# A state space block on Trainium2: the causal convolution as four shifted projections

## The chip, the core and the metric

The kernel runs on one core of one Trainium2 chip. The metric is the device time of one execution in microseconds (us); smaller is better. A core has a matrix engine (TensorE, "PE" in the profile, with "PEld" for its loading of weights), a vector engine (VectorE, "DVE"), a scalar engine (ScalarE, "ACT"), GpSimd ("POOL") and SyncE ("SP", which here issues most of the DMA transfers). Each engine works through its own queue of instructions in order; semaphores tie the queues together.

## The reference

The program is a network of four blocks on an activation `x` of shape (4, 1024, 128) in f32: four batches of 1024 tokens with 128 features. Each block is an attention-like part and a feed-forward part, each followed by `x = layernorm(x + f(x))`: block 0 is a minimal GRU with a slot feed-forward, block 1 a sparse attention with a routed feed-forward, block 2 a linear attention with a mixture of 8 experts (two per token), and block 3 a state space block with a feed-forward of 8 dense experts of hidden width 512. The change lies in block 3:

```python
def _L3_attn_ref(resid, norm_w, skip_w, in_w, conv_w, conv_b, wd1, wd2, wd2_b, wb, wc, A_log, W_D, out_w):
    ...
    x = resid * lax.rsqrt(jnp.mean(resid * resid, -1, keepdims=True) + EPS) * norm_w
    skip = x @ skip_w.T
    xe = x @ in_w.T                       # 128 features -> E = 256 channels
    xt = xe.transpose(0, 2, 1)
    xc = lax.conv_general_dilated(xt, conv_w, window_strides=(1,), padding=[(D_CONV - 1, 0)],
                                  feature_group_count=conv_w.shape[0])
    xc = xc + conv_b[None, :, None]
    xs = jax.nn.silu(xc.transpose(0, 2, 1))
    delta = jax.nn.softplus(xs @ wd1.T @ wd2.T + wd2_b)
    A = -jnp.exp(A_log)
    Bm = xs @ wb.T
    Cm = xs @ wc.T
    ...
    # for each of N = 16 states: h = exp(delta*A)*h + delta*xs*B, y = sum of h*C   (a scan over time)
    y = ys.transpose(1, 0, 2)
    y = y + xs * W_D
    y = y * jax.nn.silu(skip)
    y = y @ out_w.T
    return resid + y
```

The convolution has width 4, is causal (each output takes the token itself and the three before it, zeros ahead of the first) and depthwise: each of the 256 channels has its own four weights.

## The kernel before

**Order.** The kernel is written in the Tile framework. The Python text emits instructions in program order, interleaving several generators; a scheduler (`schedule_with_timeline_sim=True`, L2133) then fixes each engine's in-order queue from a simulated timeline. So the place of an instruction in its queue follows from what it depends on and from the durations that the scheduler assumes, not from the text alone. Only the PE order within `l2_attn` is written by hand (L962). Buffers come from pools: a tile name with `bufs=n` has n buffers used in turn, and a new tile waits until the last reader of the buffer it takes is done.

**Stages.** `Net.__init__` (L63 to L85) loads constants; the front (blocks 0 and 1, with the GRU first, its gates on ACT, its scans on DVE) takes roughly the first 620 us. `l2_attn` (L919) does the linear attention in quarters of 256 tokens with eight pairs of heads each. Its values are made in `l2_values` (L1014): for each of two 128-token chunks a tile `cv1` ("cv" in the profile) from a pool with two buffers gets a column of ones by POOL (L1019), its sums with the bias by DVE (L1029), and is then scaled by ACT (L1036) into its final form. `l2_ffn` (L1377) and `l2_combine` (L1494) are the mixture of experts of block 2, per batch: a dispatch with rows scattered into DRAM by POOL's indirect DMAs (`xrows`, L1359), tiles of tokens with their expert weights `wx` loaded by SP (L1433), and gathers of the results (`yrows` to `yg`, L1504) by POOL. They are drawn as a generator `moe` and run on into the last stage.

**The last stage, `l3` (L1549).** It works in eight halves: four batches times two halves of 512 tokens. Channels lie on partitions, in two blocks of 128 (`ec`), time lies along the free axis. A half has these steps:

- `l3_prepare` (L1652): the RMS norm of four 128x128 tiles, four transposes, an eviction by ACT with the norm's weight into `xnT` (128 features x 512 tokens, L1676). For each block one f32 matmul makes `pxe` (128 x 512 in PSUM, L1687); the helper `mm` (L127) issues every matmul, which is why so many groups carry that line. The convolution then reads `pxe`: DVE writes weight 3 times `pxe` plus the bias to `xc` (L1693) and adds the other three taps, each a `scalar_tensor_tensor` on columns shifted by 1, 2 and 3 (L1699). The three columns that the second half of a batch needs from the first are kept, already weighted, in a tile `tail` (L1697 and L1703 to L1710). All weights are halved in advance (`cw`), so that ACT's tanh (L1713, back into the PSUM bank) and one DVE operation (L1714) give the SiLU, `xs`. Two matmuls make `pdb` (64 delta features, B and C rows), which ACT evicts to `db1` (L1722) and SP writes to DRAM as `rows`; two more make `pd`, from which Exp, Ln and six-odd DVE operations make the softplus, with `ud` (delta times xs, L1748, DVE) and `dl` (delta, L1749, ACT) as results.
- `l3_scan` (L1752), for each of 16 states: SP broadcasts one row of B and one of C over 128 partitions (`bn`, `cn`, L1777); POOL multiplies `db = ud*bn` (L1782); ACT makes the decay `da` (L1786) and DVE scans `db` in place (L1787); in the first half of a batch ACT keeps the last column in `carry` (L1796); POOL multiplies `hc = db*cn` (L1798). Every second `hc` of batches 1 to 3 is added to its neighbour by an accumulating DMA that POOL issues (L1802); the rest is summed by identity matmuls into `pys`.
- `l3_sum` (L1811) and `l3_finish` (L1823): `xs` becomes `pys` plus xs times W_D (L1819), `psk` is the skip projection of the same `xnT`, `po` the output projection, then layer norm and router.
- `l3_experts` and `l3_ffn` (L1604, L1892): for each half, 8 experts of four 512-column matmuls `ph`, a ReLU `hh` on ACT (L1910), sixteen 128-column matmuls `py`, and DVE's gated sum `h_acc` (L1926). Their weights `wh` come by SP (L1639), three buffers.

`l3` weaves these: with each of the 16 scan steps of a half goes one step of the previous half's end, one step of the next half's preparation, one step of `moe`, and three or four steps of the experts. What is left of the experts runs at the very end on PE, which then has all eight PSUM banks. Before that, PSUM has one bank for each of two `pys`, two for `da`, and four under the name "ff" for everything else, `pxe`, `pdb`, `pd`, `ph` and `py` alike (L1641).

Of the kernel before, what the change touches and what calls it, by code (L numbers as in the profile page):

```python
# [18 lines left out]
P = 128  # L19
# [13 lines left out]
NH2, HD2 = 16, 64  # L33
VW = HD2 + 1
# [6 lines left out]
E3, NST, DDELTA, KCONV = 256, 16, 64, 4  # L41
# [17 lines left out]
class Net:  # L59
# [954 lines left out]
    def l2_values(self, Q):  # L1014
        nc, c2 = self.nc, self.c2
        wp = c2["wp"]
        for c in range(2):
            v1 = wp.tile([P, NH2, VW], F32, name="cv1")
            nc.gpsimd.memset(v1[:, :, HD2 : HD2 + 1], 1.0)  # L1019
            for g in range(2):  # L1020
                pv = self.psb("pj", [P, 8, HD2], "pv")
                gs = slice(g * 512, g * 512 + 512)
                self.mm(
                    pv.rearrange("p h d -> p (h d)"),
                    Q["x"][:, c * P : (c + 1) * P],
                    c2["wv"][:, gs],
                )
                hs = slice(8 * g, 8 * g + 8)
                nc.vector.tensor_add(  # L1029
                    v1[:, hs, 0:HD2],  # L1030
                    pv,
                    c2["bv"][:, gs].rearrange("p (h d) -> p h d", d=HD2),
                )
                k = Q["c0"] + c
                for i in range(2):
                    nc.scalar.activation(  # L1036
                        Q["v"][c][:, hs, i, :],
                        v1[:, hs, :],
                        AF.Copy,
                        scale=c2["trig"][:, k, i : i + 1],  # L1040
                    )
                yield
# [489 lines left out]


    def l3_load(self):
        return dict(
            wskip=self.load("s_in", [P, 2, E3]),
            we=self.load("s_e", [P, 2, ND + D]),
            wd2=self.load("s_d2", [DDELTA + 1, E3]),
            br=self.load_row("h_br", NE),
            wr=self.load("h_router", [P, NE]),  # L1540
            b2=self.load("h_b2", [NE, D]),
        )
# [6 lines left out]
    def l3(self, w3, moe, fp):  # L1549

        nc, tc, c = self.nc, self.tc, self.const
        aneg = c.tile([P, 2 * NST], F32, name="aneg")
        o = COLS["A_log"][0]
        nc.scalar.activation(aneg, self.cols[:, o : o + 2 * NST], AF.Exp)
        nc.vector.tensor_scalar_mul(aneg, aneg, -1.0)

        o, n = COLS["conv_w"][0], 2 * KCONV + 2  # L1560
        cw = c.tile([P, n], F32, name="cw")
        nc.vector.tensor_scalar_mul(cw, self.cols[:, o : o + n], 0.5)
        c3 = self.c3
        neg1 = c.tile([P, 1], F32, name="neg1")
        nc.vector.memset(neg1, -1.0)
        c3.update(w3, aneg=aneg, cw=cw, neg1=neg1)
        halves = [dict(b=b, h=h) for b in range(B) for h in range(2)]
        for i, u in enumerate(halves):
            u["prev"] = halves[i - 1] if u["h"] else None
        while "done" not in self.m2["st"][0]:  # L1570
            next(moe)
        for f in self.l3_prepare(halves[0]):
            next(moe)
        work = self.l3_experts(fp)
        c3["todo"] = []
# [24 lines left out]
        c3["all"] = True  # L1600
        for f in work:
            pass
# [49 lines left out]
    def l3_prepare(self, u):  # L1652

        nc, c3, b, h = self.nc, self.c3, u["b"], u["h"]
        sp, wp, dp = c3["sp"], c3["wp"], c3["dp"]
# [16 lines left out]
        pt = self.psb("ff", [P, 4, P], "pt")  # L1672
        for k in range(4):
            self.tr(pt[:, k, :], sq[:, k, :])
        xnT = wp.tile([P, 512], F32, name="xnT")
        nc.scalar.activation(  # L1676
            xnT, pt.rearrange("p a b -> p (a b)"), AF.Copy, scale=self.col("norm_w")
        )
        yield

        K1 = KCONV - 1
        tail = wp.tile([P, 2, K1], F32, name="tail") if h == 0 else u["prev"]["tail"]
        u["tail"] = tail
        xs = wp.tile([P, 2, 512], F32, name="xs3")
        for ec in range(2):
            p = self.psb("ff", [P, 512], "pxe")
            self.mm(p, c3["wskip"][:, 1, ec * P : (ec + 1) * P], xnT)  # L1687
            xc = sp.tile([P, 512], F32, name="xc", tag="s1")
            i = 2 * KCONV + ec
            w = [c3["cw"][:, j : j + 1] for j in range(ec * KCONV, (ec + 1) * KCONV)]  # L1690
            bias = c3["cw"][:, i : i + 1]
            o = K1 if h else 0
            nc.vector.tensor_scalar(xc[:, o:], p[:, o:], w[K1], bias, ALU.mult, ALU.add)  # L1693
            if h:
                nc.vector.scalar_tensor_tensor(
                    xc[:, 0:K1], p[:, 0:K1], w[K1], tail[:, ec, :], ALU.mult, ALU.add
                )  # L1697
            for d in range(1, KCONV):
                nc.vector.scalar_tensor_tensor(  # L1699
                    xc[:, d:], p[:, 0 : 512 - d], w[K1 - d], xc[:, d:], ALU.mult, ALU.add  # L1700
                )
            if h == 0:
                nc.vector.tensor_scalar(  # L1703
                    tail[:, ec, :], p[:, 512 - K1 :], w[0], bias, ALU.mult, ALU.add
                )
                for d in range(K1 - 1, 0, -1):
                    nc.vector.scalar_tensor_tensor(
                        tail[:, ec, 0:d], p[:, 512 - d :], w[K1 - d], tail[:, ec, 0:d],
                        ALU.mult, ALU.add,
                    )  # L1710
            yield

            nc.scalar.activation(p, xc, AF.Tanh)  # L1713
            nc.vector.scalar_tensor_tensor(xs[:, ec, :], p, 1.0, xc, ALU.add, ALU.mult)  # L1714
            yield

# [2 lines left out]
        p = self.psb("ff", [ND, 512], "pdb")  # L1719
# [23 lines left out]
        for ec in range(2):  # L1743
            p = p2[ec]
# [78 lines left out]
    def l3_finish(self, u):  # L1823


        nc, c3, b, h = self.nc, self.c3, u["b"], u["h"]
        sp, wp = c3["sp"], c3["wp"]
# [2 lines left out]
        yt = u["xs"]  # L1830
        for ec in range(2):
            p = ff([P, 512], "psk")
            self.mm(p, c3["wskip"][:, 0, ec * P : (ec + 1) * P], u["xnT"])

            t = sp.tile([P, 512], F32, name="th")
            nc.scalar.activation(t, p, AF.Tanh, scale=0.5)
            nc.vector.scalar_tensor_tensor(p, t, 1.0, p, ALU.add, ALU.mult)
            nc.vector.scalar_tensor_tensor(
                yt[:, ec, :], yt[:, ec, :], 0.5, p, ALU.mult, ALU.mult
            )  # L1840
            yield
# [18 lines left out]
        n = NC // 2  # L1860
# [89 lines left out]
    ("p_bq", 1), ("p_bk", 1), ("p_bv", 1), ("h16", 1),  # L1950
    ("f_b1", 12), ("f_b2", 2), ("f_sb2", 1),
    ("c_bq", NP2), ("c_bk", NP2),
    ("norm_w", 1), ("conv_w", 2 * KCONV), ("conv_b", 2), ("A_log", 2 * NST),
    ("one64", 1),
    ("W_D", 2),
    ("h_b1", 4 * NE),
# [1 line left out]
COLS, NCOLS = {}, 0  # L1958
# [25 lines left out]
def layout(i):  # L1984
# [5 lines left out]
    a = constants()  # L1990
    a["x"] = i["L0_attn_x"]

    cols = {}
# [7 lines left out]
    s = {k[len("L0_ffn_") :]: v for k, v in i.items() if k.startswith("L0_ffn_")}  # L2001
# [15 lines left out]
    s = {k[len("L1_attn_") :]: v for k, v in i.items() if k.startswith("L1_attn_")}  # L2017
# [6 lines left out]
    s = {k[len("L1_ffn_") :]: v for k, v in i.items() if k.startswith("L1_ffn_")}  # L2024
# [13 lines left out]
    s = {k[len("L2_attn_") :]: v for k, v in i.items() if k.startswith("L2_attn_")}  # L2038
# [23 lines left out]
    cols["one64"] = np.arange(P) == DDELTA  # L2062
    a["s_d2"] = np.concatenate([s["wd2"].T, s["wd2_b"][None, :]])
    cols["norm_w"], cols["conv_b"] = s["norm_w"], s["conv_b"]
    cols["conv_w"] = s["conv_w"].reshape(2, P, KCONV).transpose(0, 2, 1).reshape(-1)
    cols["A_log"] = s["A_log"].reshape(2, P, NST).transpose(0, 2, 1).reshape(-1)
    cols["W_D"] = s["W_D"]

# [68 lines left out]
```

## Time and profile before

Three runs took 2418.57, 2433.83 and 2437.38 us. The profiled execution is a further one.

| | |
|---|---|
| median of the three runs | 2433.83 us |
| the profiled execution's own time | 2426.07 us |
| its span in the profile | 2424.3 us, 35395 instructions |
| mean granted TensorE clock | 0.914 of full speed |
| PE busy | 2077.0 us (86%), 12170 instructions |
| PEld busy | 1456.7 us (60%) |
| DVE busy | 1439.7 us (59%), 4207 instructions |
| ACT busy | 1335.6 us (55%), 2934 instructions |
| POOL busy | 860.8 us (36%), 557 instructions |
| DMA | 209.87 MB, 75 GB/s to and from HBM over the span |

How to read what follows. The span is what the profiler's records cover; the execution's own time is 1.8 us longer. An f32 matmul leaves two matmul records and two weight loads, so counts (x) of PE are twice the matmuls in the text. Records of PE overlap their neighbours in the pipeline and their ends are modelled, so their durations add up to more than the time that PE takes for them. In the slices, the span is cut into 40 equal parts and each digit gives the busy share in tenths. A row for a window gives each engine's busy time and count, the granted clock of PE (1 is full speed), the mean busy share of the 16 DMA engines and the bytes they moved. A row of the chain of waits gives start, length, engine, what was made, the line, and a count: the chain is followed back from the last instruction to whatever released each step. A row for one instruction gives start and duration, and in brackets how long its engine stood idle before it and what ended that. A row of a tile's operations gives count, then least, median and greatest duration in ns, then the first and last start, then shapes.

### The profile page before, as it was taken

Reading aid. Unit: us, or ns where it says so; the run is one execution under the profiler, and the core shown is the slowest. Engines: PE = TensorE matmul, PEld = TensorE weight load, DVE = VectorE, ACT = ScalarE, POOL = GpSimd, SP = SyncE. Lnnn points to the kernel's source line nnn. Section 1 sums busy time; section 2 is a strip of 40 time slices with the busy share of each in tenths; the row PEclk is TensorE's granted clock in tenths of the full one; section 3 lists DMA queues with packets and bytes.
Section 4 is the critical chain, followed back from the end, with each engine's and each line's share of the span. In section 5 each row is a group of like instructions: output and inputs, shape, how many; then the busy total and the mean of one; then the engine's idle time right before and its main releaser. Section 6 shows DMA issues by size and latency. Waiting matters only on the chain. (4 is left out here: it accounts for less than half of the span.)

```text
span 2424.3 us, 35395 instructions
## 1 busy us (share of the span) xinstructions
PE 2077.0 (86%) x12170; PEld 1456.7 (60%) x12170; DVE 1439.7 (59%) x4207; ACT 1335.6 (55%) x2934; POOL 860.8 (36%) x557
## 2 busy tenths in 40 slices
PE   6767979979899999999989865776788989798988
PEld 3455655544577777787768754553455656465666
DVE  6457733433466666755656556676778777676431
ACT  6543433332456565656655555657677776666443
POOL 5001220000000011001021137868899979688500
PEclk9657969989999999999989988997999989898999
DMA  3000110013000010021222156663577766575421
GB/s 101 0 18 21 29 33 7 12 64 92 1 1 1 1 33 22 16 76 41 62 74 82 42 158 190 210 181 91 147 187 185 201 165 184 149 205 151 113 66 48
DMA packets 138517, 209.87 MB, mean 87 GB/s; under 512 B 18598, under 2 KB 75937, under 8 KB 138081
## 3 DMA queue, kind: packets, MB, share of 16 engines
q1 hardware_dynamic: 126048, 172.82, 24.0%
q0 software_dynamic: 12288, 34.79, 6.8%
q8 instruction: 96, 1.57, 0.3%
q14 instruction: 85, 0.69, 0.1%
HBM read 159.24 MB, written 23.16 MB: 75 GB/s over the span
## 5 line engine op out<-in xcount | busy, mean ns | idle before, releaser
L1798 POOL TENSOR_TENSOR hc<-db,cn 128x1024 f32<-128x1024 f32 x128 | 317.2, 2501 | 81.1 <-PE pys L127 29.7
L1782 POOL TENSOR_TENSOR db<-ud,bn 128x1024 f32<-128x1024 f32 x128 | 326.0, 2574 | 44.1 <-ACT dl L1749 16.4
L127 PEld LDWEIGHTS py<-wh,hh 128*128 128x128 f32 x2048 | 249.5, 193 | 78.2 <-issue 43.7
L127 PE MATMUL ph<-xT,wh 128*128 128x512 f32 x512 | 262.7, 632 | 24.8 <-DVE h_acc L1926 7.5
L1145 DVE SCALAR_TENSOR_TENSOR num<-po,sb_c_trig,nsin 128x65 f32<-128x65 f32 x512 | 132.7, 279 | 232.1 <-ACT nsin L1142 218.3
L127 PE MATMUL py<-wh,hh 128*128 128x128 f32 x2048 | 255.9, 277 | 13.0 <-ACT hh L1910 12.7
L1910 ACT ACTIVATE hh<-ph,sb_cols 128x512 f32<-128x512 f32 x256 | 171.1, 681 | 137.7 <-PE ph L127 111.5
L1142 ACT ACTIVATE nsin<-po,sb_c_trig 128x65 f32<-128x65 f32 x512 | 148.3, 316 | 176.7 <-DVE num L1145 103.5
L1786 ACT ACTIVATE da<-dl,aneg 128x512 f32<-128x512 f32 x256 | 175.4, 689 | 74.6 <-DVE db L1787 72.8
L1019 POOL MEMSET cv<- 128x16 f32 x32 | 4.0, 127 | 497.7 <-ACT cv L1036 354.8
L127 PE MATMUL pys<-hc,sb_c_ident 128*128 128x512 f32 x320 | 164.3, 642 | 14.7 <-DMA hc<-hc 14.7
L127 PEld LDWEIGHTS ph<-xT,wh 128*128 128x128 f32 x512 | 92.6, 201 | 117.5 <-issue 63.9
L1926 DVE SCALAR_TENSOR_TENSOR h_acc<-py,gt,h_acc 128x128 f32<-128x128 f32 x256 | 71.9, 343 | 153.0 <-PE py L127 145.3
L1787 DVE TENSOR_TENSOR_SCAN db<-da,carry,db 128x512 f32<-128x512 f32 x128 | 156.8, 1266 | 5.9 <-ACT da L1786 4.3
L1787 DVE TENSOR_TENSOR_SCAN db<-da,db 128x512 f32<-128x512 f32 x128 | 149.8, 1206 | 11.3 <-ACT da L1786 10.1
L127 PE MATMUL pqk<-xT,wE 128*128 128x256 f32 x512 | 137.0, 391 | 7.4 <-DVE cv L1029 6.0
L1359 POOL DMA_INDIRECT xrows<-xN,di x64 | 61.9, 968 | 221.2 <-ACT kN L1063 216.4
L1109 PE MATMUL po<-cv,a 128*128 128x130 f32 x1024 | 136.9, 276 | 0.9 <-DVE num L1145 0.9
L1109 PEld LDWEIGHTS po<-cv,a 128*128 128x128 f32 x1024 | 125.5, 192 | 2.6 <-issue 1.0
L1036 ACT ACTIVATE cv<-cv,sb_c_trig 128x520 f32<-128x520 f32 x128 | 86.4, 724 | 51.4 <-DVE cv L1029 46.0
L127 PEld LDWEIGHTS pys<-hc,sb_c_ident 128*128 128x128 f32 x320 | 61.1, 203 | 80.4 <-issue 59.1
L127 PEld LDWEIGHTS pqk<-xT,wE 128*128 128x128 f32 x512 | 87.9, 191 | 25.3 <-DVE cv L1029 10.1
(430 smaller groups left out, 4440.4 us busy)
## 6 DMA issues: line engine op xcount, KB each, us to landing
wx<-in_wF SPq DMA_DIRECT2D x92, 384.0 KB
wh<-in_wH SPq DMA_DIRECT2D x64, 512.0 KB
bn<-rows SPq DMA_DIRECT2D x128, 256.0 KB
cn<-rows SPq DMA_DIRECT2D x128, 256.0 KB
hc<-hc POOLq DMA_DIRECT2D x48, 512.0 KB
xrows<-zero SPq DMA_DIRECT2D x4, 1472.0 KB
xg<-xrows SPq DMA_DIRECT2D x20, 256.0 KB
yrows<-ys SPq DMA_DIRECT2D x20, 256.0 KB
```

The lines of the kernel that those rows point to most:

```text
L127: return self.nc.tensor.matmul(out=out, lhsT=lhsT, rhs=rhs, start=start, stop=stop)
L1036: nc.scalar.activation(Q["v"][c][:, hs, i, :], v1[:, hs, :], AF.Copy, scale=c2["trig"][:, k, i : i + 1],)
L1109: self.nc.tensor.matmul(out=u["po"][i][:, c, :], lhsT=u["a"][:, i, c, :], rhs=Q["v"][c][:, 2 * hp + i, :, :].rearrange("p a d -> p (a d)") ...
L1142: nc.scalar.activation(t, po[i][:, c, VW : 2 * VW], AF.Copy, scale=trig[:, k, 1:2])
L1145: nc.vector.scalar_tensor_tensor(num[:, c, i, :], po[i][:, c, 0:VW], trig[:, k, 0:1], t, ALU.mult, ALU.add)
L1359: i = nc.gpsimd.indirect_dma_start(out=rows[:, :], out_offset=bass.IndirectOffsetOnAxis(ap=st["dest"][k][:, c : c + 1], axis=0), in_=self. ...
L1782: nc.gpsimd.tensor_mul(db, ud, bc[0])
L1786: nc.scalar.activation(da, dl[:, ec, :], AF.Exp, scale=aneg[:, j : j + 1])
L1787: nc.vector.tensor_tensor_scan(db[:, ec, :], da, db[:, ec, :], carry[:, ec, n : n + 1] if h else 0.0, ALU.mult, ALU.add,)
L1798: nc.gpsimd.tensor_mul(hc, db, bc[1])
L1910: nc.scalar.activation(ht, ph, AF.Relu, bias=self.col("h_b1", i=e * NK + k))
L1926: nc.vector.scalar_tensor_tensor(acc[:, c, :], py[:, c, :], gt[:, c, e : e + 1], acc[:, c, :], ALU.mult, ALU.add,)
```

## The change

The convolution and the projection ahead of it are both linear, so tap k of the convolution can be put into the weights: for each tap, `in_w` scaled by that tap's weight per channel is a 128 x 256 matrix of its own, and `xc` is the sum of four projections of `xnT`, each shifted by one column.

- `l3_load` loads `conv_rows` (the four taps as rows of 256 channels), broadcast by SP over 128 partitions into `wconv` (128 x 4 x 256 f32, 512 KB), and four DVE operations multiply it by 0.5 and `in_w`. `l3_load` is called while `l2_attn` is emitted (L2108).
- `xnT` gets three columns ahead of its 512: for a batch's first half POOL sets them to zero, for the second ACT copies the last three columns of the half before. `tail` is gone. The skip projection `psk` reads the columns behind them.
- For each block four matmuls accumulate in one PSUM bank, on `xnT[:, k:k+512]` for k = 0 to 3; ACT evicts the bank to `xc` with the halved bias (Identity), and tanh and the SiLU's product follow as before. The generator's step that stood between the convolution and tanh now stands behind tanh.
- `cw` (10 columns) becomes `cb` (2 columns), the packed constants `cols` lose the 8 columns of `conv_w`, and `cv1` of `l2_values` gets one buffer in place of two.

```diff
--- before.py
+++ after.py
@@ -1015,7 +1015,7 @@
         nc, c2 = self.nc, self.c2
         wp = c2["wp"]
         for c in range(2):
-            v1 = wp.tile([P, NH2, VW], F32, name="cv1")
+            v1 = wp.tile([P, NH2, VW], F32, name="cv1", bufs=1)
             nc.gpsimd.memset(v1[:, :, HD2 : HD2 + 1], 1.0)
             for g in range(2):
                 pv = self.psb("pj", [P, 8, HD2], "pv")
@@ -1532,8 +1532,19 @@
 
 
     def l3_load(self):
+        w = self.load("s_in", [P, 2, E3])
+
+        wconv = self.const.tile([P, KCONV, E3], F32, name="wconv")
+        self.nc.sync.dma_start(
+            out=wconv, in_=self.io["conv_rows"].to_broadcast([P, KCONV, E3])
+        )
+        for k in range(KCONV):
+            self.nc.vector.scalar_tensor_tensor(
+                wconv[:, k, :], wconv[:, k, :], 0.5, w[:, 1, :], ALU.mult, ALU.mult
+            )
         return dict(
-            wskip=self.load("s_in", [P, 2, E3]),
+            wskip=w[:, 0:1, :],
+            wconv=wconv,
             we=self.load("s_e", [P, 2, ND + D]),
             wd2=self.load("s_d2", [DDELTA + 1, E3]),
             br=self.load_row("h_br", NE),
@@ -1557,13 +1568,13 @@
         nc.scalar.activation(aneg, self.cols[:, o : o + 2 * NST], AF.Exp)
         nc.vector.tensor_scalar_mul(aneg, aneg, -1.0)
 
-        o, n = COLS["conv_w"][0], 2 * KCONV + 2
-        cw = c.tile([P, n], F32, name="cw")
-        nc.vector.tensor_scalar_mul(cw, self.cols[:, o : o + n], 0.5)
+        o = COLS["conv_b"][0]
+        cb = c.tile([P, 2], F32, name="cb")
+        nc.vector.tensor_scalar_mul(cb, self.cols[:, o : o + 2], 0.5)
         c3 = self.c3
         neg1 = c.tile([P, 1], F32, name="neg1")
         nc.vector.memset(neg1, -1.0)
-        c3.update(w3, aneg=aneg, cw=cw, neg1=neg1)
+        c3.update(w3, aneg=aneg, cb=cb, neg1=neg1)
         halves = [dict(b=b, h=h) for b in range(B) for h in range(2)]
         for i, u in enumerate(halves):
             u["prev"] = halves[i - 1] if u["h"] else None
@@ -1672,45 +1683,34 @@
         pt = self.psb("ff", [P, 4, P], "pt")
         for k in range(4):
             self.tr(pt[:, k, :], sq[:, k, :])
-        xnT = wp.tile([P, 512], F32, name="xnT")
+
+        K1 = KCONV - 1
+        xnT = wp.tile([P, K1 + 512], F32, name="xnT")
+        if h == 0:
+            nc.gpsimd.memset(xnT[:, 0:K1], 0.0)
+        else:
+            nc.scalar.copy(xnT[:, 0:K1], u["prev"]["xnT"][:, 512:])
         nc.scalar.activation(
-            xnT, pt.rearrange("p a b -> p (a b)"), AF.Copy, scale=self.col("norm_w")
-        )
-        yield
-
-        K1 = KCONV - 1
-        tail = wp.tile([P, 2, K1], F32, name="tail") if h == 0 else u["prev"]["tail"]
-        u["tail"] = tail
+            xnT[:, K1:], pt.rearrange("p a b -> p (a b)"), AF.Copy, scale=self.col("norm_w")
+        )
+        yield
+
         xs = wp.tile([P, 2, 512], F32, name="xs3")
         for ec in range(2):
             p = self.psb("ff", [P, 512], "pxe")
-            self.mm(p, c3["wskip"][:, 1, ec * P : (ec + 1) * P], xnT)
+            for k in range(KCONV):
+                self.mm(
+                    p,
+                    c3["wconv"][:, k, ec * P : (ec + 1) * P],
+                    xnT[:, k : k + 512],
+                    k == 0,
+                    k == K1,
+                )
             xc = sp.tile([P, 512], F32, name="xc", tag="s1")
-            i = 2 * KCONV + ec
-            w = [c3["cw"][:, j : j + 1] for j in range(ec * KCONV, (ec + 1) * KCONV)]
-            bias = c3["cw"][:, i : i + 1]
-            o = K1 if h else 0
-            nc.vector.tensor_scalar(xc[:, o:], p[:, o:], w[K1], bias, ALU.mult, ALU.add)
-            if h:
-                nc.vector.scalar_tensor_tensor(
-                    xc[:, 0:K1], p[:, 0:K1], w[K1], tail[:, ec, :], ALU.mult, ALU.add
-                )
-            for d in range(1, KCONV):
-                nc.vector.scalar_tensor_tensor(
-                    xc[:, d:], p[:, 0 : 512 - d], w[K1 - d], xc[:, d:], ALU.mult, ALU.add
-                )
-            if h == 0:
-                nc.vector.tensor_scalar(
-                    tail[:, ec, :], p[:, 512 - K1 :], w[0], bias, ALU.mult, ALU.add
-                )
-                for d in range(K1 - 1, 0, -1):
-                    nc.vector.scalar_tensor_tensor(
-                        tail[:, ec, 0:d], p[:, 512 - d :], w[K1 - d], tail[:, ec, 0:d],
-                        ALU.mult, ALU.add,
-                    )
-            yield
+            nc.scalar.activation(xc, p, AF.Identity, bias=c3["cb"][:, ec : ec + 1])
 
             nc.scalar.activation(p, xc, AF.Tanh)
+            yield
             nc.vector.scalar_tensor_tensor(xs[:, ec, :], p, 1.0, xc, ALU.add, ALU.mult)
             yield
 
@@ -1830,7 +1830,7 @@
         yt = u["xs"]
         for ec in range(2):
             p = ff([P, 512], "psk")
-            self.mm(p, c3["wskip"][:, 0, ec * P : (ec + 1) * P], u["xnT"])
+            self.mm(p, c3["wskip"][:, 0, ec * P : (ec + 1) * P], u["xnT"][:, KCONV - 1 :])
 
             t = sp.tile([P, 512], F32, name="th")
             nc.scalar.activation(t, p, AF.Tanh, scale=0.5)
@@ -1950,7 +1950,7 @@
     ("p_bq", 1), ("p_bk", 1), ("p_bv", 1), ("h16", 1),
     ("f_b1", 12), ("f_b2", 2), ("f_sb2", 1),
     ("c_bq", NP2), ("c_bk", NP2),
-    ("norm_w", 1), ("conv_w", 2 * KCONV), ("conv_b", 2), ("A_log", 2 * NST),
+    ("norm_w", 1), ("conv_b", 2), ("A_log", 2 * NST),
     ("one64", 1),
     ("W_D", 2),
     ("h_b1", 4 * NE),
@@ -2062,7 +2062,7 @@
     cols["one64"] = np.arange(P) == DDELTA
     a["s_d2"] = np.concatenate([s["wd2"].T, s["wd2_b"][None, :]])
     cols["norm_w"], cols["conv_b"] = s["norm_w"], s["conv_b"]
-    cols["conv_w"] = s["conv_w"].reshape(2, P, KCONV).transpose(0, 2, 1).reshape(-1)
+    a["conv_rows"] = s["conv_w"].reshape(1, E3, KCONV).transpose(0, 2, 1)
     cols["A_log"] = s["A_log"].reshape(2, P, NST).transpose(0, 2, 1).reshape(-1)
     cols["W_D"] = s["W_D"]
 
```

More of the change, by code (lines that the diff above doesn't have):

```diff
@@ L1686, in l3_prepare @@
             p = self.psb("ff", [P, 512], "pxe")
-            self.mm(p, c3["wskip"][:, 1, ec * P : (ec + 1) * P], xnT)
-            xc = sp.tile([P, 512], F32, name="xc", tag="s1")
-            i = 2 * KCONV + ec
-            w = [c3["cw"][:, j : j + 1] for j in range(ec * KCONV, (ec + 1) * KCONV)]
-            bias = c3["cw"][:, i : i + 1]
-            o = K1 if h else 0
-            nc.vector.tensor_scalar(xc[:, o:], p[:, o:], w[K1], bias, ALU.mult, ALU.add)
-            if h:
-                nc.vector.scalar_tensor_tensor(
-                    xc[:, 0:K1], p[:, 0:K1], w[K1], tail[:, ec, :], ALU.mult, ALU.add
-                )
-            for d in range(1, KCONV):
-                nc.vector.scalar_tensor_tensor(
-                    xc[:, d:], p[:, 0 : 512 - d], w[K1 - d], xc[:, d:], ALU.mult, ALU.add
-                )
-            if h == 0:
-                nc.vector.tensor_scalar(
-                    tail[:, ec, :], p[:, 512 - K1 :], w[0], bias, ALU.mult, ALU.add
-                )
-                for d in range(K1 - 1, 0, -1):
-                    nc.vector.scalar_tensor_tensor(
-                        tail[:, ec, 0:d], p[:, 512 - d :], w[K1 - d], tail[:, ec, 0:d],
-                        ALU.mult, ALU.add,
-                    )
+            for k in range(KCONV):
[6 more added lines that the diff above has]
+                )
+            xc = sp.tile([P, 512], F32, name="xc", tag="s1")
+            nc.scalar.activation(xc, p, AF.Identity, bias=c3["cb"][:, ec : ec + 1])
+            nc.scalar.activation(p, xc, AF.Tanh)
             yield
-            nc.scalar.activation(p, xc, AF.Tanh)
             nc.vector.scalar_tensor_tensor(xs[:, ec, :], p, 1.0, xc, ALU.add, ALU.mult)
```

## The prediction

> **What bounds the kernel now.** First the page's slices: which engine is full where.
>
> ```profile
> PE   6767979979899999999989865776788989798988
> ...
> DVE  6457733433466666755656556676778777676431
> ...
> POOL 5001220000000011001021137868899979688500
> ```
>
> A slice is 60.6 us. The change lies in `l3_prepare`, which first runs at 1411 us (slice 24). There no row is at 9: PE 5, DVE 6, POOL 7, then all rise together. I cut the stage into windows at the first multiply of each of the eight scans (the times POOL starts `db<-ud,bn` with a fresh half):
>
> ```profile
> core 0: us, PE busy (x) PEld busy (x) DVE busy (x) ACT busy (x) POOL busy (x), PEclk, DMA share, GB/s
> 1411.00:1477.00 66.00, 32.52 (x140) 24.14 (x141) 31.06 (x101) 30.48 (x70) 30.80 (x33) 0.68 0.51 151
> ...
> 1883.00:1983.00 100.00, 94.42 (x455) 60.77 (x454) 75.70 (x147) 71.14 (x132) 87.67 (x45) 0.96 0.71 191
> ...
> 2090.00:2190.00 100.00, 89.29 (x413) 55.87 (x412) 70.78 (x131) 65.08 (x115) 80.84 (x40) 0.93 0.66 172
> ...
> 2284.00:2424.30 140.30, 124.32 (x693) 89.10 (x692) 33.38 (x119) 55.94 (x88) 0.00 (x0) 0.96 0.18 53
> ```
>
> In the second and third half of the stage (1477 to 1700, same view) PE is busy 67 of 94 and 96 of 129 us, a quarter idle. From 1883 it is idle 6 to 11 us in 100, with DVE near 71 to 76. Is that PE really full, or are its modelled ends flattering it? The chain of waits decides:
>
> ```profile
> 2244.50 2.95 PE py L127 x26
> 2247.45 1.72 PE ph L127 x4
> 2249.17 0.45 PE py L127 x4
> 2249.61 1.72 PE pys L127 x4
> ```
>
> It runs from matmul to matmul without a gap: 1.72/4 = 0.43 us for each 512-column record, and 2.95/26 = 0.113 us for a 128-column one. An instruction is two records (1024 `py` instructions, 2048 records), so a 512-column f32 matmul takes PE 0.86 us, not the 0.59 to 0.64 us of its row. With these prices the window 2090 to 2190 holds 64 `ph`, 48 other 512-column, 256 `py` and about 45 small records: 27.5 + 20.6 + 28.9 + 6 = 83 us at full clock, 83/0.93 = 89 us. PE is full there by its own issue rate.
>
> **What is removed and added in `l3_prepare`** (8 halves, 16 column blocks):
>
> ```profile
> L1699 DVE SCALAR_TENSOR_TENSOR xc<-pxe,cw,xc x48: 720/743/751, 1418.6 to 2157.1; 128x511 f32<-128x511 f32 x16, 128x510 f32<-128x510 f32 x16, 128x509 f32<-128x509 f32 x16
> ...
> L127 PE MATMUL pxe<-xnT,sb_s_in x32: 592/592/1061, 1416.1 to 2151.8; 128*128 128x512 f32 x32
> L1693 DVE TENSOR_SCALAR xc<-pxe,cw x16: 776/805/811, 1417.3 to 2152.4; 128x512 f32<-128x512 f32 x8, 128x509 f32<-128x509 f32 x8
> ```
>
> DVE loses 16 x 0.80 + 48 x 0.74 + 2.2 + 3.5 + 1.7 (the 3-column tails at 0.27, 0.22, 0.21) = 55.7 us, 7 a half. PE gains 3 instructions for each of 16 blocks: 48 x 0.86 = 41.3 us, 5.16 a half at full clock. ACT gains 16 Identity evictions; nearest row L1722 (97x512 from PSUM, 0.67 us): 10.7 us, and four 3-column copies at 0.19 (L1796). POOL gains four memsets (0.13 each in L1019's row).
>
> Here a rule is weighed. The Trainium skill, "Perfetto Trace Analysis", section "Identifying the Most-Contended Engine", says matmul busy share misjudges TensorE, that the share of weight loading shows its headroom, while for VectorE occupancy is fair. By that rule the window 2090 to 2190 has PEld at 56 of 100 and DVE at 71: PE would take 5.2 us for nothing, DVE would be the fuller one and give back up to 7, so five halves would gain some 20 to 35 us and the median would come near 2400. By the chain row PE cannot take anything for nothing: +5.16/0.93 = 5.5 us a half. I go with the row, because the chain names PE back to back and in that window PE waits for DVE for 3.4 us only (`pmv` 3.0, `h_acc` 0.4).
>
> **Half by half.** The queue orders of both programs can be compared without a run. On PE the four `pxe` of a block stand where the one stood: in halves 5 to 7 each `pxe`, `pdb` and `pd` has the same number of `ph` and `py` ahead of it as before. So the shorter DVE chain does not let a half's preparation overtake; all that follows on PE is pushed.
>
> - Halves 5, 6, 7 (prepared 1883 to 2190): 3 x 5.5 = +16.6 us in full.
> - Halves 3, 4: PE idles 16.5 and 12.3 us and POOL is about as full. I count half: 2 x 5.16 x 0.5/0.95 = +5.4 (bounds 0 and 11).
> - Relief on DVE in these five: PE waits there for `h_acc`, `gt`, `xs` some 11 us in all; a third goes, -4. A `pxe` bank (one of four `ff` banks) is also held about 4 us instead of 11.
> - The boundary before half 5: before, `ud` stands on DVE ahead of the two `xs<-xs,pys` (L1819), which wait for an accumulating DMA; after, behind them, as it already does at halves 6 and 7. There the profile shows POOL without work:
>
> ```profile
> 2190.16 9.24 POOL L1782 TENSOR_TENSOR db<-ud,bn 128x1024 f32<-128x1024 f32 x4 [13.26 <-ACT dl L1749]
> ```
>
>   At half 5 the wait was 3.2; it becomes about 13. POOL loses 10, of which PE, which sets the end, feels about half: +5 (0 to 10).
> - Half 0, exposed, nothing else covers it. DVE's in-order queue mixed `xc` with the dispatch of batch 3 and stopped 3.4 us for a tanh that was late on ACT:
>
> ```profile
> 1428.99 0.69 DVE L1714 SCALAR_TENSOR_TENSOR xs<-pxe,xc 128x512 f32<-128x512 f32 x1 [3.37 <-ACT pxe L1713]
> ...
> 1441.09 2.02 PE L127 MATMUL pdb<-xs,sb_s_e 128*97 128x512 f32 x2 [7.13 <-DVE xs L1714]
> ```
>
>   After, both `xs` can be ready near 1426 instead of 1441. But on POOL 32 indirect DMAs (1.25 us each, 40 us) stand ahead of the first multiply, and start at about 1423 to 1425 in both, so it starts near 1466 rather than 1476.8: 10 us. Part is lost again, as POOL in the new order reaches the gathers of batch 2 (1556 before) sooner than their rows, last written at 1549. I take -8 (0 to -20). Halves 1 and 2: PE has 27 and 33 us idle, 0.
>
> Sum in this stage: +16.6 + 5.4 - 4 + 5 - 8 = +15. The tail from 2284, all PE, has the same instructions in the same order: 0; it starts later by the sum.
>
> **What moves elsewhere.** The weights: a 512 KB load is one more issue on SP (0.43 us) and four 128x256 products on DVE, 4 x 0.41 (row of L1469) = 1.7 us. The scheduler puts both in the first 30 us, before the fifth GRU gate or so, in place of `sidx`, `gate_d` and `onehot` (1.6 us and a 1.2 us DMA wait), which go behind the GRU. DVE is nearly without a gap from 24 us. If the weights land late, the GRU's scans and, behind them, its matmuls and ACT gates wait; `sidx_i` took 3.2 us from issue to use, and one more 512 KB at the 300 GB/s of that stretch takes 1.7: between -2 and +3 us; I take 0.
>
> `cv1` gets one buffer: the memset (POOL) and the bias add (DVE, ahead of PE's `pqk`) of the next chunk wait for the last two scalings (ACT, 1.35 us) of this one. In the trace those end at 772.74 and the next add is at 776.45: 3.7 us of cover, without which each of 16 quarters would lose up to 1.5 us on PE. Only the first quarter runs its chunks back to back (631 to 641): +1. POOL's new order keeps each memset ahead of its add.
>
> Total +16 us: 2424.3 + 16 = 2440 for the span. The profiled run (2426.07) is 7.8 us under the median of the three, 2433.83, so the median goes to 2450.
>
> **Rivals.**
> 1. The matmuls are hidden: the late halves go at POOL's pace (80 to 88 us busy and eight DMA issues in 94 to 107). For it: POOL's stretches of 2.3 us steps with no gap. Against it: POOL's own waits are on PE (`hc<-PE pys` 29.7 us in the stage). Then only half 0's gain and the small costs remain: 2427 to 2438, say 2434.
> 2. Faster: DVE sets the early pace. One place, 1411 to 1700: if DVE's 14 us in halves 1 and 2 and the 14 us POOL stood for `DVE db` at 1600 vanish as well as the 10 at half 0, the stage gains 25 to 38 against +23 late: 2420 to 2433, say 2427. It decides once the third half starts before 1676 (1700 now); below 2410 only if the rule above held as well.
> 3. More slower: the gathers of batch 2 and the scans of half 0, now in fours (`db` x4, `hc` x4), block POOL 20 to 30 us: nothing gained early, +24 for the rest, +20: 2478. For it: these gathers were ready only 7 us before POOL came to them. Against it: the dispatch that feeds the experts comes earlier too.
>
> **Chances.** Forecast 0.50 (its own range 2438 to 2466), hidden 0.24, faster 0.12, more slower 0.14. About 1% (24 us) is what a measurement of this kernel can tell from none. Slower by over 1% (above 2458): 0.17 from the forecast and 0.13 from rival 3, 0.30; faster (under 2410): 0.07, the rest of rival 2 falls within; same 0.63. Range for 8 in 10: 2418 to 2482: rival 1 and 2 inside at the low end, rival 3 at the high.
>
> **What would show it.** `pxe` 128 records, none of L1693 or L1699; PE busy up some 50 us and DVE down 54. Right: windows of halves 5 to 7 longer by 5 to 6 us each (boundary 5 more), tail 140 us, first multiply near 1466. Wrong: those windows unchanged with PE busy at 95, rival 1; the third half starting before 1676, rival 2; POOL waiting over 10 us for `yrows` or `DVE db` before 1700, rival 3; a shift before 1411 of over 4 us, an error in the weights or `cv1`.

## The result and the profile after

| | before | changed |
|---|---|---|
| median of 15 runs each | 2427.47 us | 2443.57 us |
| ratio, with its 95% interval | 1 | 1.0058 [1.0044, 1.0072] |
| the profiled execution's own time, span | 2426.07, 2424.3 us | 2437.26, 2435.5 us |

The ratio times 2427.5 is +14 us [10.7, 17.5], a little slower and within 1%. Against the median of 15 the sum's +16 is 2443, where the medians have 2443.57; the 2450 was 16 on the median of three runs, which lay higher. The sum held, but in part by luck: several of its terms were off by more than half the total and the errors offset each other. The experiments are about that.

The slices of the changed kernel, 60.9 us each:

```profile
PE   6677879979899999999989957775889989898988
...
DVE  7548643433566666755565536666777656666431
...
POOL 5001210000000011001021147877988959778500
```

From slice 29 on PE is at 8 or 9 throughout, DVE no longer above 7. The same four windows as before, each moved to its own landmark (stage start; first multiply of halves 4 and 5; of 6 and 7; start of the tail):

```profile
core 0: us, PE busy (x) PEld busy (x) DVE busy (x) ACT busy (x) POOL busy (x), PEclk, DMA share, GB/s
1403.00:1469.00 66.00, 33.69 (x148) 23.77 (x148) 25.82 (x87) 30.52 (x69) 30.44 (x32) 0.71 0.46 143
1886.00:1994.50 108.50, 99.22 (x480) 63.10 (x478) 69.24 (x137) 73.84 (x136) 81.95 (x41) 0.99 0.65 176
2096.70:2201.20 104.50, 93.92 (x426) 58.93 (x424) 65.75 (x121) 66.98 (x118) 81.20 (x40) 0.92 0.60 164
2290.70:2435.50 144.80, 129.24 (x697) 92.34 (x696) 34.24 (x120) 56.03 (x88) 0.00 (x0) 0.94 0.17 52
```

From the first `pxe` to the first multiply of half 0 it is 61.3 us (1407.9 to 1469.2), and was 60.7: nothing was gained ahead of the first scan. The second and third are 9 and 4 us longer, but the stretch between them, from the first multiply of half 5 to that of half 6, is 4.8 us shorter (102.1, was 106.9). The chain of waits is matmul to matmul again, at the same prices:

```profile
2229.38 0.86 PE psk L127 x2
2230.24 2.90 PE py L127 x26
2233.14 1.72 PE ph L127 x4
2234.86 1.72 PE pys L127 x4
```

And the tile's rows show what was exchanged, 128 records for 32, ACT's eviction, and none of the DVE chain:

```profile
L127 PE MATMUL pxe<-xnT,wconv x128: 590/592/1190, 1407.9 to 2163.4; 128*128 128x512 f32 x128
L1710 ACT ACTIVATE xc<-pxe,cb x16: 667/678/688, 1413.7 to 2164.1; 128x512 f32<-128x512 f32 x16
```

Set side by side at landmarks (stage start by the first `pxe`; first multiplies of halves 0, 3, 5, 6, 7; end), the changed profile stands at -8.2, -7.6, -2.5, +11.8, +7.0, +11.1 and +11.2 us to the one before. So it arrived early, lost 5.7 up to half 3 and 13.7 from there to the end. These are differences of one execution against one other; what the change costs is read from the runs below.

### The profile page after: what moved, and what is told of

The parts are those of the page before. It is cut to its first block, busy times and chain, and to the rows that moved or that the text cites. A ratio compares the mean times of both kernels' runs of the same rounds, so it can differ in the third digit from the quotient of the medians.

```text
span 2435.5 us, 35528 instructions
## 1 busy us (share of the span) xinstructions
PE 2094.6 (86%) x12266; PEld 1467.0 (60%) x12266; DVE 1395.9 (57%) x4115; ACT 1343.4 (55%) x2954; POOL 860.7 (35%) x561
## 5 line engine op out<-in xcount | busy, mean ns | idle before, releaser
L127 PE MATMUL pys<-hc,sb_c_ident 128*128 128x512 f32 x320 | 158.8, 620 | 6.9 <-DMA hc<-hc 6.9
L1787 DVE TENSOR_TENSOR_SCAN db<-da,db 128x512 f32<-128x512 f32 x128 | 149.2, 1207 | 21.2 <-ACT da L1786 15.5
L127 PEld LDWEIGHTS pqk<-xT,wE 128*128 128x128 f32 x512 | 88.1, 191 | 27.9 <-DVE cv L1029 12.9
L131 PE MATMUL pt<-sb_c_ident,xN 128*128 128x128 f32 x224 | 55.4, 353 | 54.7 <-ACT xN L174 33.3
```

What stands on the lines that cost most here:

```text
L127: return self.nc.tensor.matmul(out=out, lhsT=lhsT, rhs=rhs, start=start, stop=stop)
L1787: nc.vector.tensor_tensor_scan(db[:, ec, :], da, db[:, ec, :], carry[:, ec, n : n + 1] if h else 0.0, ALU.mult, ALU.add,)
```

## The experiments

Each of three groups (e1 to e4, e5 to e8, e9 to e12) ran beside the kernel before on one chip. The time in the last column is the ratio's distance from 1 times the median of before in that group (2427.87, 2423.12, 2424.00), with its 95% interval. A comparison across groups sets two such differences side by side. The changed kernel itself, in its own comparison, stands at +14.1 [10.7, 17.5]. e4, e6 and e11 leave taps of the convolution out and e9 and e10 leave scatters out, so these five do not compute the whole block.

| run | median us | against before, us |
|---|---|---|
| e1 halves 0 to 3 by matmuls | 2439.93 | +10.7 [7.3, 14.1] |
| e2 halves 4 to 7 by matmuls | 2440.21 | +12.1 [7.0, 17.0] |
| e3 weights and `cv1` alone | 2426.24 | -1.9 [-4.6, +1.0] |
| e4 change with one tap, three left out | 2411.26 | -18.9 [-25.0, -12.9] |
| e5 before, 48 matmuls more | 2436.10 | +15.3 [8.7, 21.6] |
| e6 change with two taps, two left out | 2415.47 | -8.2 [-11.9, -4.4] |
| e7 before, first tap on ACT | 2447.95 | +24.5 [18.7, 30.5] |
| e8 change, taps in bf16 | 2419.92 | -2.7 [-6.3, +0.7] |
| e9 change, 15 scatters left out | 2418.94 | -5.1 [-8.7, -1.7] |
| e10 before, 15 scatters left out | 2415.65 | -8.7 [-12.4, -5.3] |
| e11 before, one DVE tap, three left out | 2420.41 | -3.4 [-6.5, -0.2] |
| e12 change, both projections bf16 | 2411.96 | -11.4 [-15.0, -7.8] |

### Which halves cost, and what the weights cost: e1, e2, e3

```diff
 # e1: on_pe = b < 2     e2: on_pe = b >= 2     (the two branches in words)
+if on_pe: four matmuls per block, eviction by ACT, tanh, xs
+else:     one matmul per block and the DVE chain with tail, as before
 # e3: the kernel before, with l3_load of the change (wconv unread) and
-            v1 = wp.tile([P, NH2, VW], F32, name="cv1")
+            v1 = wp.tile([P, NH2, VW], F32, name="cv1", bufs=1)
```

> The first two batches (halves 0 to 3) use four matmuls, the last two (halves 4 to 7) the convolution on DVE as before; weights and cv1 as in the change. By the prediction's sum: half 0 -8, half 3 half of 5.4 for it alone, i.e. +3, cv1 and weights +1, so 4 us under the kernel before (about -4). By the rival read from the two traces (the early gain is swallowed at the scatter of batch 3 and lost in POOL's new order; the order of the front gains 3): -3 in the front, +5 to +10 in halves 0 to 3, so +2 to +7 over before. If nothing early matters, about -3.

> The other way round: halves 0 to 3 on DVE, halves 4 to 7 by four matmuls. By the prediction's sum: halves 5 to 7 +16.6, half 4 +3, DVE relief -4, boundary +5, cv1 and weights +1: about +21 over before. By the rival read from the traces (halves 4 to 7 cost some 8 to 10 in all, the front gains 3): +5 to +8.

> The kernel before, with one buffer for cv1 and with the 512 KB of taps loaded and multiplied into weights that nothing reads; the convolution stays on DVE in all halves. By the prediction +1 (-2 to +4). By the rival that the reordered front is 3 us shorter: -3. The stage from 1411 us should have the lengths of before.

e3: -1.9, so weights and `cv1` cost nothing that can be measured. In the two profiles the changed kernel reached the stage 8.2 us early; most of that is one execution against another. Kernels whose program ahead of this stage is that of before came to the last attention chunks at -1.7 (e5), +4.0 (e7), +2.4 (e10) and -6.4 us (e11) in their profiles, counted from the profile before. A gain of a few us in the front, inside the interval of e3, is not excluded. A shift of 6 us far from the change needs runs, not a profile.

e1 refutes the prediction's early part: not -4 but +10.7. e2 came to +12.1, not +21: late halves cost less than the sum had. Over e3 the early halves alone cost 12.6, the late ones alone 14.0, together 26.6, where all eight cost 16.0. The four intervals leave some 7 us either way, so the two parts cost less together than singly, by 10.6 us, just clear of noise. Why is not shown. It means that the 14 us cannot be split into an early and a late share: with the late halves changed already the early ones add 2 (14.1 - 12.1), with the early ones changed the late ones add 3 (14.1 - 10.7), each with 5 or 6 us either way.

### What a matmul costs, what DVE's relief is worth: e4, e5, e6, e11

```diff
 # e4: range(K1, KCONV), e6: range(2, KCONV) in the change
-            for k in range(KCONV):
+            for k in range(K1, KCONV):
 # e5, in the kernel before
-            self.mm(p, c3["wskip"][:, 1, ec * P : (ec + 1) * P], xnT)
+            for k in range(KCONV):
+                self.mm(p, c3["wskip"][:, 1, ec * P : (ec + 1) * P], xnT)
 # e11, in the kernel before: only the first tensor_scalar on xc is kept, over all
 # 512 columns; the `tail` operations go too (shortened here)
-            for d in range(1, KCONV):
-                nc.vector.scalar_tensor_tensor(...)
```

> The changed kernel with only the last tap's matmul in each block, so three taps of the convolution are left out; ACT's eviction and the missing DVE chain stay. It shows what the 48 extra matmuls cost. By the prediction: 16.6 + 5.4 = 22 us under the changed kernel, about 6 to 8 under before. By the rival that PE hides much of them: only 8 to 10 under the changed kernel, about +5 over before.

> The kernel before with its projection issued four times into the same bank (the same values each time), the convolution still on DVE: the 48 extra matmuls alone, with no relief on DVE. If the terms add (48 matmuls cost 32 us between e4 and the changed kernel, the DVE chain and the front are worth 17 to 19): +32 over before. By the prediction's price (22 us in halves 3 to 7, nothing before): +22 to +27. If DVE, kept full, hides PE's extra work: under +15.

> The changed kernel with only the last two taps' matmuls (two taps of the convolution are left out). If every matmul costs the same, 16 more than in e4 cost 32/3 = 11 us: about 6 us under before (2422). If the first extra matmul in a block is hidden, as e4 (2411). If one full-rate threshold decides, nearer the changed kernel (2440).

> The kernel before with only the first of its four convolution operations (three taps and the tails left out): DVE loses 42.9 us, PE and ACT nothing. Independent of the changed kernel's ACT eviction and its front. If relief on DVE is what e4 gained (17 to 19 us under before for 55.7): 13 to 15 under before. If e4's gain was the shorter path through ACT or the front's order: within 5 of before.

The 48 matmuls alone (e5): +15.3, or 0.32 us each of the 0.86 that the chain charges. In the changed form the ladder from one to two to four taps costs 10.7 for 16 and 22.3 for 32 more: 0.67 and 0.70 us each. Its three rungs come from three comparisons, which leave some 7 and 5 us either way, so only the second is clear of the 0.32. Relief on DVE alone (e11) gives 3.4 for 42.9 us of DVE work: nearly all of that work was beside the path. 15.3 and -3.4 add to +12 (7 either way), which agrees with the change's +14.

e4 does not fit that sum. With the same matmuls as before and 12.8 us less DVE work than e11 it is 15.5 us quicker than e11, of which the front of e3 is 2. So the +12 is not the whole account: the changed form has a gain of its own, and its matmuls then cost more than those of e5 (33.0 for 48, the ladder's two steps together). What else differs is ACT's eviction in place of a DVE operation, the step's place behind tanh, and the queue orders that follow. No run separates these; the remaining 13.6 us (7 either way) stay open.

### The same tap on ACT: e7

```diff
-            nc.vector.tensor_scalar(xc[:, o:], p[:, o:], w[K1], bias, ALU.mult, ALU.add)
+            nc.scalar.activation(xc[:, o:], p[:, o:], AF.Identity, bias=bias, scale=w[K1])
```

> The kernel before with only the first of the four convolution operations moved from DVE to ACT (Identity with scale and bias, 16 times), no matmul added. DVE loses 16 x 0.80 = 12.9 us of the 55.7. If the gain of e4 (17 us under before for 55.7 us less on DVE, 10.7 more on ACT) is in proportion: 4 us under before. If it is the whole chain's length in each half that counts, or the bank's early release: 0 to -2. If ACT is as full as DVE: 0 to +4.

It took 24.5 us more, on the wrong side of every expectation. Who DVE waited for among the operations of `xc`, with total and times:

```profile
its engine sat idle before it (us, times) until:
  ACT xc L1693: 24.2, 12
```

The tap moved, the other three stayed behind it, and DVE stood 24.2 us for ACT, where the kernel before has no such wait: the chain now goes PE, ACT, DVE, ACT, DVE. That the wait makes all of the 24.5 is inferred; no run takes it away. The change moves the whole convolution off DVE and has no such pair of crossings.

### Where half 0's gain went: e9, e10

The prediction had `xs` ready near 1426 rather than 1441. It was: DVE's queue in the changed kernel (start, duration, operation, idle time before it and what ended it):

```profile
1415.07 0.69 DVE L1714 SCALAR_TENSOR_TENSOR xs<-pxe,xc 128x512 f32<-128x512 f32 x1 [4.24 <-ACT pxe L1712]
1425.02 0.69 DVE L1714 SCALAR_TENSOR_TENSOR xs<-pxe,xc 128x512 f32<-128x512 f32 x1 [3.19 <-ACT yg L1522]
...
1447.87 0.42 DVE L1466 SCALAR_TENSOR_TENSOR sg<-sg,ph 128x256 f32<-128x256 f32 x1 [18.08 <-issue]
```

Then nothing for 18 us. PE stood as well:

```profile
1452.71 1.12 PE L131 MATMUL pt<-sb_c_ident,xg 128*128 128x128 f32 x4 [19.60 <-ACT ys L1485]
```

In that time POOL issued the 16 scatters of batch 3 (`xrows`, 1429.9 to 1449.8). SP stood too: it issued no transfer from 1433.3 to 1452.4, and its queue moved no packet from 1436.2 to 1453.4. Then three engines start in the same moment:

```profile
1452.39 0.36 SPq L1433 DMA_DIRECT2D wx<-in_wF  x1
1452.39 0.27 ACT L1485 COPY ys<-py 128x128 f32<-128x128 f32 x1 [4.56 <-remote]
1452.39 0.42 DVE L1469 SCALAR_TENSOR_TENSOR mh<-sg,ph 128x256 f32<-128x256 f32 x1 [4.10 <-remote]
```

Bytes moved from 1425 to 1475 in the changed kernel, 1.25 us a column:

```profile
GB/s 59 52 107 291 280 292 347 379 303 59 52 52 52 52 52 52 52 52 52 59 52 0 47 269 250 169 106 337 46 67 200 304 388 398 364 374 308 147 8 231
```

From about 1436 to 1451 it is 52 GB/s: 65 KB in 1.25 us, one scatter of 128 rows of 512 bytes, and hardly anything else. Before, the same stall lay at 1454.5 to 1467.1, under scatters at 1449 to 1469, after `xs`:

```profile
1467.06 2.07 PE L127 MATMUL ph<-xgT,wx 128*128 128x128 f32 x8 [12.54 <-issue]
```

In the twelve profiles with all 16 scatters PE has its longest idle time of that stretch, 10 to 20 us, under them or from their last moments on (in e11 from 1.6 us behind them). PE, ACT and DVE stand all together for 4 to 13 us of it in one piece, so the "14 to 20 us together" in the expectation of e9 is too much. Both kernels lose it, and the earlier `xs` ran into it. e9 and e10 leave out 15 of the 16 scatters (batch 3's rows stay zero in block 2's experts):

```diff
+                if b == 3 and put:
+                    yield
+                    continue
                 i = nc.gpsimd.indirect_dma_start(out=rows[:, :],
```

> The changed kernel without 15 of the 16 scatters of batch 3 (its rows for the experts of block 2 stay zero). In all nine profiles so far PE, ACT and DVE stand still for 14 to 20 us together while those 16 indirect transfers are issued, wherever they lie. If the scatter makes the stall: PE's gap near 1433 to 1452 shrinks to under 5, the first multiply of half 0 comes 15 to 30 us earlier than in the changed kernel (19 of it POOL's own issue time), and where the late halves are PE's, most of 15 stays to the end: 2425 to 2430. If the stall has another cause (weights late on SP): the gap stays and only POOL's 19 go. If early time is given back later anyway: 2440.

> The same 15 scatters left out of the kernel before. If the scatter makes the stall: its gap at 1454 to 1467 goes, and without it the convolution's exposed chain at half 0 (xs at 1429 and 1441) sets the first multiply; the difference between e9 and this is then the change with the stall out of the way: by the prediction's half 0 (-8 of gain) the change would cost 6 to 8 us in place of 14. If half 0 is worth nothing even so: 14 to 16.

The first multiply of half 0 in e9, the change:

```profile
1451.91 2.36 POOL L1785 TENSOR_TENSOR db<-ud,bn 128x1024 f32<-128x1024 f32 x1
```

and in e10, the kernel before:

```profile
1467.83 2.35 POOL L1785 TENSOR_TENSOR db<-ud,bn 128x1024 f32<-128x1024 f32 x1 [14.29 <-DVE ud L1751]
```

POOL stands 14.29 us in e10 for the exposed chain and not at all in e9. PE's longest idle time there is 5.0 us in e9 and 7.13 in e10, and that one is `pdb` on `xs`, as it was before. SP's queue is without a packet for 3.5 us at most around it in e9, where it was 17.2 in the changed kernel. The scatters made the stall. (Both runs spare POOL its 19 us of issuing as well; between them that cancels.) e9 came out at 2419, under the 2425 to 2430 expected of it; some 3 of that is the lower median of before in its group. With the stall gone the change costs 8.7 - 5.1 = 3.6 us (5 either way by the two intervals) in place of 14: some 10 us of gain (6 either way) exist and are hidden by the scatters. The profiles put them at half 0: its first multiply is 15.9 us earlier in e9 than in e10, 6.6 of it because the stage was reached earlier (-4.2 and +2.4 us to before), 9 within it. What inside the scatters holds the engines (their own instructions late, weights behind them on the queues) no run here tells; that SP issues no transfer itself, and that three engines start together, suggests one common cause rather than one late load.

### Matmuls at a quarter of the price: e8, e12

```diff
+        wb = wconv.bitcast(BF16)      # products are written in place, as bf16
+        xnB = wp.tile([P, K1 + 512], BF16, name="xnB")   # e8: beside xnT
 # e12: xnT is left out, psk reads xnB and a bf16 copy of its weights
```

> The changed kernel with the four taps' weights and a second copy of xnT in bf16 for the convolution only (skip projection and all else stay f32; ACT has one more 128x512 eviction a half). No row of a bf16 matmul is in the traces so far. If one takes a single record of 0.43 us, the 64 cost 27.5 us at full clock against 13.8 in e4 and 55 in the changed kernel: one third of the way from e4, 2411 + 11 = 2422. If it takes half of that, PE has what it has in e4: 2411 to 2415, under both kernels. If PE's matmul price is not what costs the 32 us, as the changed kernel, 2440.

> As e8, with the skip projection in bf16 too, on the same bf16 xnT: one ACT eviction a half less than e8 (5.5 us of ACT), and 16 matmuls of 0.86 us become 16 of the bf16 kind (one record each, 0.38 in its row). e8 stood at 2420 with before at 2423. If PE sets the late halves: 16 x (0.86 - 0.3) = 9 us less, 75% of it seen, so about 2413, under both kernels. If not, 2420.

PE's queue in e8, four taps of one block between f32 work:

```profile
2127.80 1.03 PE L128 MATMUL pxe<-xnB,wconv 128*128 128x512 bf16 x4
2128.67 0.83 PE L128 MATMUL py<-wh,hh 128*128 128x128 f32 x6
```

From start to the next start it is 0.87 us for four, 0.22 each, against 0.86 in f32. The change's matmuls then cost PE what the one f32 projection did. e8 is 17 us under the changed kernel and within noise of before. (Its profiled execution, 2405.46, is the shortest of 22, so its windows are not read.) e12, with one eviction less and the skip projection cheap too, is 11.4 under before and 25 under the change: of the kernels that compute the whole block it is the quickest, at the price of bf16 rounding of the inputs and weights of these two projections.

## Why the prediction was right, step by step

- **What bounds the late stage.** Right in kind: matmuls cost, DVE's relief does not pay. By the rule that the prediction weighed, weight loading as PE's headroom, PE at 56 of 100 would have taken the matmuls for nothing and the median come near 2400; they cost 15 us even with DVE untouched (e5). DVE's occupancy promised up to 35 us; relief there was worth 3.4 (e11). By occupancy POOL, at 81 and 88 of 100, was fuller than DVE anyway. But "cannot take anything for nothing" was too strong: the 48 matmuls have 41 us of issue time and cost 15. The prediction's own sum fills 89 us of 100, and its chain of waits begins at 2176 us, so it says nothing of the windows 1883 to 2176 by itself.
- **Halves 5 to 7, +16.6, and halves 3 and 4, +5.4.** The mechanism stands, the size was too large: with relief and boundary the sum had +23 from half 3 on, the profile has 13.7 and e2 measures +12.1 for halves 4 to 7. In the profile the three stretches are 9.2 longer, 4.8 shorter and 4.1 longer, not 5 to 6 longer each. The step that failed is "in full" at the chain's price: 0.86 us is what PE takes when it is back to back, and it is not so all the time (waits for `hc<-hc`, `gT` and `hh` remain), so a matmul cost 0.32 to 0.70. The granted clock works against the difference in the second window, 0.99 against 0.96 before: there it makes the changed kernel quicker.
- **DVE relief, -4.** Near in size to e11, -3.4 [-6.5, -0.2], though that is for all eight halves.
- **Boundary before half 5, +5.** The order and the stall came as said, POOL's wait went from 3.17 to 20.20:

```profile
1982.83 9.25 POOL L1782 TENSOR_TENSOR db<-ud,bn 128x1024 f32<-128x1024 f32 x4 [3.17 <-ACT dl L1749]
1994.58 2.33 POOL L1782 TENSOR_TENSOR db<-ud,bn 128x1024 f32<-128x1024 f32 x1 [20.20 <-DVE pmv L159]
```

  But PE did not feel half of it. Before, it had waited there for `hc<-hc` itself, as the next two rows show. In the changed kernel it no longer did; its waits there, for `gT`, `h_acc` and `dl`, come to 4.2:

```profile
1980.34 3.78 PE L127 MATMUL pys<-hc,sb_c_ident 128*128 128x512 f32 x4 [4.28 <-DMA hc<-hc]
1986.40 3.78 PE L127 MATMUL pys<-hc,sb_c_ident 128*128 128x512 f32 x4 [2.28 <-DMA hc<-hc]
```

  Its next half's experts started 1.7 us earlier than before (1991.96, was 1993.70), and the next stretch is the one that got 4.8 us shorter. e3 has the same order, with the convolution on DVE, and the same stall (17.11), and its runs show no loss. No cost of this term can be seen.
- **Half 0, -8.** Failed. `xs` came early as predicted; the first multiply came at 1469 not 1466, and that only because the stage began 8.2 us sooner. The sum moved POOL's gathers and scatters earlier and did not ask what the other engines do while the scatters run, although the profile before shows PE idle 12.54 us under them. With the scatters left out of both kernels (e9, e10) the gain is there, some 10 us.
- **Halves 1 and 2, 0.** Too low where the early halves are changed alone: e1 has +10.7 for halves 0 to 3. In the changed kernel's profile the stretch from half 0's to half 2's first multiply is 10.4 us longer and the next one 5.3 shorter. POOL's new order waits more often in the gathers of batches 2 and 3, for `m_acc` 24.4 us in the stage where it was 5.2; that is rival 3's mechanism, smaller than it claimed; that it makes the loss is not tested.
- **Weights and `cv1`, 0 and +1.** No cost to be seen (e3: -1.9 [-4.6, +1.0]). The sign that was to betray an error here, a shift of over 4 us before 1411, came up all the same, and e3 shows that one profile cannot tell it.
- **Tail, 0.** The window is 144.8 us, was 140.3. The granted clock is 0.94 in place of 0.96. In the changed kernel's profile consecutive `pxe` records start 0.43 us apart where the granted clock is 1 and 0.85 apart where it is 0.5, so PE's time goes with the inverse of the clock: 140.3 become 143.3, and four `pys` records that now fall into it take 1.7. The work itself is the same.
- **What the views were to show.** DVE fell by 43.8 us, not 54, and PE rose by 17.6, not 50. The rows' durations overlap their neighbours' by about 0.1 us, and the clock, 0.920 against 0.914, takes by the same rule some 14 us off the rest of PE (2077 x 0.0065). The 96 new records are 41 us by their issue time; less 14 that would be 27, and the remaining 10 stay open.

In the profile, then, an early term 14 too low, a late one 9 too high and an arrival 9 sooner than the +1 summed met in +11 where 16 was forecast. That the number came out is luck in this part; that it came out slower, by matmuls on PE that DVE's relief does not pay for, is not (e5, e11). The rivals: hidden is out as a whole (e5 pays 15 of its 41 us of issue time, and the ratio's interval is clear of 1); faster is out, the third half began at 1702, not before 1676; more slower happened in part.

## What to carry to other kernels

Moving work from one engine to another is paid for out of what the receiving engine's own chain can spare; the sending engine's occupancy said little here, where 43 us less on DVE bought 3. Before you book a gain from an earlier chain, look at what it will run into: a stall that was behind the chain can come to lie in front of it. When PE must take more work, ask for its price in the narrower type first: four bf16 taps cost one f32 projection.

## What was not expected

- While sixteen scatters are issued back to back PE stands 10 to 20 us, with ACT, DVE and SP beside it for a good part of that, and the queues move 52 GB/s. Leaving 15 of them out is worth 8.7 us to the kernel before and 19 to the changed one.
- One DVE operation in four moved to ACT, 0.77 us there, cost 24.5 us over 16 blocks, 1.5 us each time.
- A program that is the same ahead of the stage arrived there between -6.4 and +4.0 us of the profile before. In one piece of the front (312 to 345 us) the granted clock was 0.50 before, and between 0.50 and 0.93 in the changed kernel, some 4 us.
